# Two transformer layers on one core: the border from layer 0 to layer 1, with unordered scatters per expert, a separate pool for expert outputs, token loads moved ahead of list set-up, and first roots taken tile by tile

## The chip, the cores and the metric

The kernel runs on one core of a Trainium2 chip. A core has five engines that each work through a list of instructions of their own, in order: TensorE (PE in the profile; its weight loads are PEld), VectorE (DVE), ScalarE (ACT), GpSimd (POOL) and SyncE (SP, here only an issuer of transfers). They wait for each other through semaphores. Transfers run on 16 DMA engines; those that SP issues are in the profile's queue q1, those that POOL issues (the indirect ones, which take row numbers from memory) in q0. SBUF is the on-chip memory, PSUM the memory that TensorE writes to.

The metric is device time in microseconds (us). The kernel before takes 3005.03 us, the median of three runs (3000.24, 3005.03 and 3007.15).

## The reference, cut to what matters

`x` is 4096 tokens (2 x 2048) of 512 numbers in f32. Two layers follow each other; each is an attention to a short context and then a mixture of experts.

```python
x = x + attention_0(layernorm(x), ctx)            # 16 heads, 154 context rows
# layer 0, experts: each of 8 experts picks its 1024 best tokens
xf = layernorm(x).reshape(-1, 512)
scores = softmax(xf @ router_w + router_b)
G, idx = top_k(scores.T, 1024)                    # per expert
h1 = relu(xf[idx] @ w1 + b1)                      # 512 -> 2048
eo = h1 @ w2 + b2                                 # 2048 -> 512
y = zeros_like(xf).at[idx.reshape(-1)].add((eo * G[..., None]).reshape(-1, 512))
x = x + y
x = x + attention_1(layernorm(x), ctx)            # one head, 154 context rows
# layer 1, experts: each token picks 2 of 8 experts, plus a shared one
x = x + shared(layernorm(x)) + routed(layernorm(x))
```

A token can be picked by several experts of layer 0, but by one expert at most once.

## The kernel before, in words

The kernel is one program in four stages: attention of layer 0; choice of tokens and experts of layer 0; attention, shared expert and routing of layer 1; routed experts of layer 1. The change touches the end of the second stage and the start of the third.

**Experts of layer 0.** A block is half the tokens of one expert, 512 of them, so there are 16 blocks `b`. `hidden(b)` computes the first product, `outputs(b, b2_bc)` the second, both in a scheme that gets each pair of 2 x 2 block products from seven products and extra additions. `product` emits the matmuls (L709). While it emits them it counts ticks, and `after(n, fn)` puts other work into the engines' lists n ticks later; so the code itself fixes each engine's order (the stage is under a manual schedule for TensorE, DVE, ACT and POOL). SP is not in it: its order comes from the scheduler.

`outputs` works in two passes `p`, each of which makes two tiles of 128 tokens in one buffer `eo` of two halves (tag "eo", two buffers, in the pool `sm`). The last product of a pass, `p4`, completes tile `p + 2`. `finish` adds the bias `b2` on POOL (L928), scales by the gate on ACT three ticks later (`scale`, L895), and scatters two ticks after that (`scatter`, L900): an indirect transfer on POOL's queue that adds 128 rows of 2 KB to the rows of `xacc` in device memory that `idx` names. `xacc` holds the residual stream. Because all scatters write the same tensor, each one waits until the one before it has landed.

**The border.** When the pools of layer 0 close, their SBUF is given to the pools of layer 1, and a tile of layer 1 waits for whatever last used its place. SP then issues, in this order: seven loads that layer 1 needs throughout (L1046 to L1059: `kw`, `vp`, the two parts of `wsr`, `sb1_bc`, `ws2`, `sb2_bc`; here called the preloads), six small transfers that initialise rows of zeros and empty lists (L1090, L1093, L1097), and the tokens `x2[t]` from `xacc`, 256 KB a tile (`load`, L1135). Between them come the weights of the routed experts (`load_routed`, into `wall`), an expert per four steps. Each of SP's transfers uses one of eight semaphores in turn, and waits until the transfer eight places before it has landed.

**Attention and routing of layer 1.** `step(s)` emits the work of one step for a pipeline over 32 tiles; s runs from -10. A tile's layer norm is taken in three places: `stats(t)` on DVE (L1150, L1151) gives mean and variance; `roots(m)` takes the square root (ACT, L1156) and the reciprocal (DVE, L1157) for four tiles at a time; `norm3(t)` normalises (POOL, L1164). For the first four tiles that is `roots(-1)` in step -4, after all four statistics. Then TensorE transposes the tile (L1120), ACT copies it (L1122), TensorE computes the scores (`scores1`, L1172), and DVE takes their minimum (L1177), the first work of the step's softmax. The functions of ACT come in tables, and a change of table is an instruction of its own (ACT_TABLE_LOAD).

The set-up of the lists (`zrow`, `rank_of`, `io_p`, `ids`, `region`, `unused`, `csum`, `tri1`) stands before the steps: counters on POOL, conversions and zeros on DVE, and the six small transfers. `zrow` shares the tag "xn3" with the normalised tiles, which have two buffers.

Of the kernel before, what the change touches and what calls it, by code (L numbers as in the profile page):

```python
# [20 lines left out]
P = 128  # L21
# [3 lines left out]
TB = 512  # L25
# [30 lines left out]
def two_layers(ctx: ExitStack, tc: tile.TileContext, a, out):  # L56
# [66 lines left out]
    with (  # L123
# [373 lines left out]
    with tc.tile_pool(name="wm", bufs=4) as wm:  # L497
# [188 lines left out]
        HD2 = D // 2  # L686
        with (
            tc.tile_pool(name="sm", bufs=2) as sm,
            tc.tile_pool(name="pm", bufs=2, space=PSUM) as pm,
# [5 lines left out]
            def after(n, fn, *args):  # L695

                due.setdefault(now[0] + n, []).append((fn, args))
# [196 lines left out]
            def scale(eo, gate):  # L894
                nc.scalar.mul(eo, eo, gate)  # L895

            def scatter(b, t, eo):
                e, half = divmod(b, CAP // TB)
                col = half * TPB + t
                nc.gpsimd.indirect_dma_start(  # L900
                    out=xacc[:, :],
                    out_offset=bass.IndirectOffsetOnAxis(ap=idx[:, e, col : col + 1], axis=0),
                    in_=eo,
                    in_offset=None,
                    compute_op=ALU.add,
                )

            def outputs(b, b2_bc):
                e, half = divmod(b, CAP // TB)
                w2v = [blocks_of_w2(e, q) for q in range(4)]  # L910
                hsum = {}

                def hs(p, i):
# [13 lines left out]
                def finish(t, eo):  # L927
                    nc.gpsimd.tensor_tensor(eo, eo, b2_bc, ALU.add)  # L928
                    after(3, scale, eo, gates.pop((b, t)))
                    after(5, scatter, b, t, eo)  # L930

# [13 lines left out]
                for p in range(2):  # L945
# [3 lines left out]
                    def p_(h, m):  # L949
                        return product([[(h[:, j], m(j // 2)[:, j % 2]) for j in range(JF)]])[:, 0]  # L950
# [4 lines left out]
                    def w2t(i):  # L955
                        return lambda q: t2w[e, q][:, i]

                    u1, u2, u3, u23 = u_tiles(1)
                    u1, u2, u3, u23 = u1[:, 0], u2[:, 0], u3[:, 0], u23[:, :, 0]
                    eo = sm.tile([P, 2, D], F32, tag="eo", name="eo", bufs=2)  # L960
                    p1 = p_(a11, w2b(0))
# [70 lines left out]
    with ExitStack() as outer:  # L1032
# [42 lines left out]

        zrow = sf1.tile([P // 2, D], F32, tag="xn3", name="zrow")
        nc.vector.memset(zrow, 0.0)

        def iota1(shape, pattern, base_, mult, name):
            i = sf1.tile(shape, I32, tag=name + "_i", name=name + "_i", bufs=1)  # L1080
            nc.gpsimd.iota(i, pattern=pattern, base=base_, channel_multiplier=mult)
            f = wf.tile(shape, F32, name=name)
            nc.vector.tensor_copy(f, i)
            return f

        rank_of = iota1([P, E], [[-1, E]], E, 0, "rank_of")
        io_p = iota1([P, 1], [[1, 1]], 0, 1, "io_p")
        ids = iota1([P, SPLIT, 2], [[2 * P, SPLIT], [1, 2]], 0, 2, "ids")
        for G_ in groups:
            nc.sync.dma_start(G_.xn[G_.n : G_.n + P // 2, :], zrow)  # L1090
            G_.region = iota1([P, E], [[G_.n, E]], 0, 0, f"region{G_.g}")
            unused = iota1([2 * E, P], [[1, P]], 2 * G_.n, P, f"unused{G_.g}")
            nc.sync.dma_start(  # L1093
                G_.lists[0 : G_.rows, :].rearrange("(e r) c -> e r c", e=E),
                unused[0:E].unsqueeze(1).to_broadcast([E, G_.n // P, P]),
            )
            nc.sync.dma_start(G_.lists[G_.rows : G_.rows + E, :], unused[E : 2 * E])  # L1097
            G_.csum = wf.tile([P, E], F32, name=f"csum{G_.g}")
            nc.vector.memset(G_.csum, 0.0)
        tri1 = wf.tile([P, P], F32, name="tri1")  # L1100
        nc.gpsimd.affine_select(
            tri1, ones, pattern=[[1, P]], compare_op=ALU.is_gt, fill=0.0, base=0, channel_multiplier=-1
        )
        rank_bc = rank_of.unsqueeze(1).to_broadcast(SH)

        def first_highest(v, m, oh):

            m2 = sf.tile([P, TPB, 1], F32, tag="fh_m", name="fh_m")
            nc.vector.tensor_reduce(m, v, AX.X, ALU.max)
            nc.vector.tensor_tensor(oh, v, m.to_broadcast(SH), ALU.is_equal)  # L1110
            nc.vector.tensor_tensor(oh, oh, rank_bc, ALU.mult)
            nc.vector.tensor_reduce(m2, oh, AX.X, ALU.max)
            nc.vector.tensor_tensor(oh, oh, m2.to_broadcast(SH), ALU.is_equal)
# [45 lines left out]

        def norm3(t):  # L1160
            blk, i = divmod(t, TPB)
            mv, rstd, _ = event(blk - 1)
            x3n[t] = sf1.tile([P, D], F32, tag="xn3", name="xn3")
            nc.gpsimd.tensor_scalar(  # L1164
                x3n[t], x2[t], mv[:, 1, i, 0:1], rstd[:, 1, i : i + 1], ALU.subtract, ALU.mult
            )

# [184 lines left out]
        def block_of(m):  # L1352
            return 0 <= m < NB

        def step(s):
# [59 lines left out]
        def table(G_):  # L1415
# [16 lines left out]
            first = small([P, E], F32, "first")  # L1432
            nc.vector.tensor_scalar(past, end, io_p, None, ALU.is_le)
            nc.vector.tensor_tensor(first, past, n_t, ALU.mult)
# [3 lines left out]
            nc.vector.tensor_reduce(ex[:, 1:2], first, AX.X, ALU.add)  # L1438
            nc.vector.tensor_tensor(ex[:, 2:3], io_p, ex[:, 1:2], ALU.subtract)
            nc.vector.scalar_tensor_tensor(  # L1440
# [3 lines left out]

            nc.vector.tensor_scalar_add(ex[:, 3:4], io_p, float(G_.rows - 2 * G_.n // P))
            nc.vector.tensor_tensor(ex[:, 3:4], ex[:, 3:4], past[:, E - 1 : E], ALU.mult)
# [245 lines left out]
```

## Time and profile before

| What | Value |
|---|---|
| median of three runs | 3005.03 us |
| the profiled execution's own time | 3016.07 us |
| its span, first to last instruction | 3014.4 us |
| mean granted TensorE clock | 0.966 |
| TensorE busy (matmul) | 2778.1 us, 92% |
| DVE busy | 1547.0 us, 51% |
| POOL busy | 1216.7 us, 40% |
| ACT busy | 880.1 us, 29% |
| scatters to xacc | 64, of 1.57 us on POOL each, from 797.4 to 2312.8 us |

A line of the timeline gives the start, the length, the engine, the source line, the operation with "output <- input" by the program's names, the shapes and the count; in brackets stands how long the engine was idle before it and who released it. A line of the chain that ended last gives start, length and the work that the chain went through there. An engine's idle time matters only where that engine, or what waits for it, is on the path that sets the end. All times of a trace are counted from the start of the span.

### The profile page before, as it was taken

The numbers are of one execution on the slowest core, as the hardware profiler recorded it, in microseconds if no ns is written. First come the engines' busy times: TensorE is split into PE (matmuls) and PEld (weight loads), VectorE is DVE, ScalarE is ACT, GpSimd is POOL, SyncE is SP. The second block draws the span as 40 slices with busy tenths as digits, with TensorE's granted clock in tenths as the row PEclk, the third lists the DMA queues.
The fourth block names the chain that finished last, engine by engine and source line by source line (L and its number), as shares of the span: only waits on it lengthen the run. The fifth ranks groups of instructions, "written<-read, shape, count | busy, mean of one in ns | idle before, by whom it ended". The sixth has DMA issues, their size and how long they took to land. (4 is left out here: it accounts for less than half of the span.)

```text
span 3014.4 us, 38792 instructions
## 1 busy us (share of the span) xinstructions
PE 2778.1 (92%) x14262; PEld 2133.2 (71%) x14262; DVE 1547.0 (51%) x2933; ACT 880.1 (29%) x1854; POOL 1216.7 (40%) x986
## 2 busy tenths in 40 slices
PE   7889998867999999999999999999995888889995
PEld 4444554445888888888888888888885655567773
DVE  4677776544545435444454355443532555544355
ACT  2555554411122112212122112211220555432331
POOL 1445544403344424343334333432431555465552
PEclk9899999878999999999999999999998999899998
DMA  4011111161122231231222312312113642143387
GB/s 160 18 36 46 47 61 47 53 219 38 25 77 84 44 111 25 78 86 27 67 81 70 88 22 78 88 29 85 56 15 80 220 81 64 47 92 129 133 315 282
DMA packets 127083, 256.47 MB, mean 85 GB/s; under 512 B 16508, under 2 KB 22668, under 8 KB 126742
## 3 DMA queue, kind: packets, MB, share of 16 engines
q1 hardware_dynamic: 93232, 170.79, 16.9%
q0 software_dynamic: 29056, 74.81, 10.8%
q10 hardware_dynamic: 4608, 8.39, 0.7%
q8 instruction: 115, 1.88, 0.3%
q14 instruction: 72, 0.59, 0.1%
HBM read 176.09 MB, written 77.85 MB: 84 GB/s over the span
## 5 line engine op out<-in xcount | busy, mean ns | idle before, releaser
L831 ACT ACTIVATE H<-H,b_sb 128x256 f32<-128x256 f32 (+1 forms) x384 | 198.9, 571 | 563.0 <-DVE H L882 287.0
L928 POOL TENSOR_TENSOR eo<-eo,b_bc 128x512 f32<-128x512 f32 x64 | 96.4, 1506 | 647.4 <-DVE eo L974 585.4
L709 PE MATMUL prod<-w2q,H 128*128 128x256 f32 x1536 | 346.9, 379 | 0.0
L709 PEld LDWEIGHTS prod<-w2q,H 128*128 128x128 f32 x1536 | 289.5, 190 | 38.1
L312 POOL TENSOR_TENSOR pr<-pr,sm 128x616 f32<-128x616 f32 x128 | 155.2, 1213 | 275.5 <-DVE sm L311 249.7
L709 PE MATMUL prod<-xsum,sw 128*128 128x256 f32 x1024 | 245.4, 380 | 0.7 <-DVE xsum L792 0.7
L709 PE MATMUL prod<-xgT,w1q 128*128 128x256 f32 x1024 | 243.2, 380 | 0.0
L709 PE MATMUL prod<-xgT,sw 128*128 128x256 f32 x1024 | 243.1, 380 | 0.0
L709 PE MATMUL prod<-tw,hs 128*128 128x256 f32 x1024 | 234.5, 380 | 0.0
L817 POOL TENSOR_TENSOR sw<-w1q 128x512 f32<-128x512 f32 x128 | 189.6, 1481 | 84.3 <-PE prod L709 84.0
L709 PEld LDWEIGHTS prod<-xgT,w1q 128*128 128x128 f32 x1024 | 195.5, 191 | 26.8
L709 PEld LDWEIGHTS prod<-tw,hs 128*128 128x128 f32 x1024 | 192.8, 190 | 27.8 <-PE prod L709 2.5
L709 PEld LDWEIGHTS prod<-xsum,sw 128*128 128x128 f32 x1024 | 193.3, 190 | 26.7 <-POOL sw L817 1.0
L709 PEld LDWEIGHTS prod<-xgT,sw 128*128 128x128 f32 x1024 | 193.4, 190 | 25.7
L113 ACT COPY xgT<-pt 128x512 f32<-128x512 f32 x64 | 37.5, 585 | 431.7 <-PE pt L112 431.7
L900 POOL DMA_INDIRECT xacc<-eo,idx x64 | 100.6, 1572 | 153.0 <-DMA xacc<-eo,idx 92.1
L1513 PE MATMUL ph<-xgT,wc 128*128 128x128 f32 x1248 | 152.6, 275 | 7.4 <-DVE wc L1503 6.0
L289 DVE TENSOR_REDUCE mx<-sc 128x4 f32<-128x616 f32 x128 | 101.8, 795 | 105.5 <-PE sc L285 103.5
L1513 PEld LDWEIGHTS ph<-xgT,wc 128*128 128x128 f32 x1248 | 145.6, 192 | 9.0 <-issue 5.3
L1528 PE MATMUL po<-wall,h1r 128*128 x312 | 146.7, 593 | 1.7 <-issue 1.7
L1536 DVE TENSOR_TENSOR y<-po,wall 128x512 f32<-128x512 f32 x78 | 53.9, 691 | 144.1 <-PE po L1528 134.1
L1485 POOL DMA_INDIRECT xg<-xn,xrow x78 | 84.1, 1079 | 106.6 <-PE pt L1120 100.6
(296 smaller groups left out, 5156.9 us busy)
## 6 DMA issues: line engine op xcount, KB each, us to landing
w1q<-in_w SPq DMA_DIRECT2D x32, 1024.0 KB
w2q<-in_w SPq DMA_DIRECT2D x32, 1024.0 KB
y<-ys SPq DMA_DIRECT2D x40, 256.0 KB
xs<-row SPq DMA_DIRECT2D x32, 260.0 KB
x_sb<-in_x SPq DMA_DIRECT2D x32, 256.0 KB
x<-in_x SPq DMA_DIRECT2D x32, 256.0 KB
xacc<-x SPq DMA_DIRECT2D x32, 256.0 KB
x<-xacc SPq DMA_DIRECT2D x32, 256.0 KB
```

The lines of the kernel that those rows point to most:

```text
L113: nc.scalar.copy(dstT[:, :, ts(t, P)], pt)
L289: nc.vector.tensor_reduce(mx, sc[:, :, 0:TKV], AX.X, ALU.min)
L312: nc.gpsimd.tensor_tensor(pr, pr, sm.to_broadcast([P, 4, TKV]), ALU.mult)
L709: nc.tensor.matmul(ps[:, g, :], w, m, start=i == 0, stop=i == len(terms) - 1)
L817: nc.gpsimd.tensor_tensor(o, l, m, ALU.add if i == 0 else ALU.subtract)
L831: nc.scalar.activation(dst, src, AF.Relu, bias=b1_sb[:, e, f : f + 1])
L900: nc.gpsimd.indirect_dma_start(out=xacc[:, :], out_offset=bass.IndirectOffsetOnAxis(ap=idx[:, e, col : col + 1], axis=0), in_=eo, in_offse ...
L928: nc.gpsimd.tensor_tensor(eo, eo, b2_bc, ALU.add)
L1485: nc.gpsimd.indirect_dma_start(out=xg[r], out_offset=None, in_=G_.xn[:, :], in_offset=bass.IndirectOffsetOnAxis(ap=G_.xrow[:, i : i + 1], ...
L1513: nc.tensor.matmul(ph[:, c, :], wc[:, k * HE + c * P : k * HE + (c + 1) * P], x_[:, k, :], start=k == 0, stop=k == KC - 1,)
L1528: nc.tensor.matmul(po_[r], h[:, c, :], wflat[:, bass.ds(at + (W2_AT + c * D), D)], start=c == 0, stop=c == HE // P - 1)
L1536: nc.vector.tensor_tensor(y, po_.pop(r), wflat[:, bass.ds(at + B2_AT, D)], ALU.add)
```

## The change

1. *Scatters without order.* The scatters of one expert are declared free of dependences among each other. The scatter follows sooner: scaling after two ticks and scatter after three, in place of three and five, so that on POOL a tile's scatter stands before the other tile's bias add.
2. *Own memory.* `eo` moves from the pool `sm` to a pool of its own, `se`, that is opened first.
3. *The last tile of layer 0.* In the last pass of the last block, `finish_early` adds the bias and scales both finished parts (the right half of `eo`, and `u3`) before the last product; the last product's output is scaled and added to `u3` by one DVE instruction, and the scatter follows. A one-element memset of POOL stands between the last two scatters.
4. *Tokens first.* The set-up of the lists becomes a function, `lists_init`, that is called in step -4, after ten token loads and part of a weight load have been issued. `zrow` moves to the tag "xn4", and "xn3" gets three buffers.
5. *First roots tile by tile.* `first_tiles` takes statistics, root, reciprocal and normalisation of tiles 0 to 3 one after the other; the first three are normalised on DVE in place of POOL. A square root of one element (`warm`) ahead of the steps brings in the table.

The diff without what only moves or is re-indented:

```diff
         with (
+            tc.tile_pool(name="se", bufs=2) as se,
             tc.tile_pool(name="sm", bufs=2) as sm,
...
             def scatter(b, t, eo):
...
-                nc.gpsimd.indirect_dma_start(
+                sc_ = nc.gpsimd.indirect_dma_start(
...
+                tc.declare_no_dep(sc_.ins, group=f"xacc{e}", reason="an expert's tokens differ")
+                tc.add_to_no_dep_group(f"xacc{e}", sc_.ins)
...
                 def finish(t, eo):
                     nc.gpsimd.tensor_tensor(eo, eo, b2_bc, ALU.add)
-                    after(3, scale, eo, gates.pop((b, t)))
-                    after(5, scatter, b, t, eo)
+                    after(2, scale, eo, gates.pop((b, t)))
+                    after(3, scatter, b, t, eo)
+
+                def finish_early(eo, u3):
+
+                    gate = gates[b, TPB - 1]
+                    nc.vector.tensor_tensor(eo[:, HD2:D], eo[:, HD2:D], b2_bc[:, HD2:D], ALU.add)
+                    nc.vector.tensor_tensor(u3, u3, b2_bc[:, 0:HD2], ALU.add)
+                    scale(eo[:, HD2:D], gate)
+                    scale(u3, gate)
...
-                    eo = sm.tile([P, 2, D], F32, tag="eo", name="eo", bufs=2)
+                    eo = se.tile([P, 2, D], F32, tag="eo", name="eo")
...
-                    p4 = p_(a22, w2t(2))
-                    nc.vector.tensor_tensor(eo[:, 1, left], p4, u3, ALU.add)
-                    after(1, finish, p + 2, eo[:, 1])
+                    if last and p == 1:
+                        finish_early(eo[:, 1], u3)
+                        p4 = p_(a22, w2t(2))
+                        gate = gates.pop((b, TPB - 1))
+                        nc.vector.scalar_tensor_tensor(eo[:, 1, left], p4, gate, u3, ALU.mult, ALU.add)
+
+                        after(1, nc.gpsimd.memset, se.tile([P, 1], F32, name="pad", bufs=1), 0.0)
+                        after(1, scatter, b, TPB - 1, eo[:, 1])
+                    else:
+                        p4 = p_(a22, w2t(2))
+                        nc.vector.tensor_tensor(eo[:, 1, left], p4, u3, ALU.add)
+                        after(1, finish, p + 2, eo[:, 1])
...
-        zrow = sf1.tile([P // 2, D], F32, tag="xn3", name="zrow")
-        nc.vector.memset(zrow, 0.0)
...
+        def lists_init():
+            nonlocal rank_of, io_p1, ids, tri1
+            zrow = sf.tile([P // 2, D], F32, tag="xn4", name="zrow", bufs=3)
+            nc.vector.memset(zrow, 0.0)
...
-        def norm3(t):
+        def norm3(t, eng=nc.gpsimd):
             blk, i = divmod(t, TPB)
             mv, rstd, _ = event(blk - 1)
-            x3n[t] = sf1.tile([P, D], F32, tag="xn3", name="xn3")
...
+            x3n[t] = sf1.tile([P, D], F32, tag="xn3", name="xn3", bufs=3)
+            eng.tensor_scalar(x3n[t], x2[t], mv[:, 1, i, 0:1], rstd[:, 1, i : i + 1], ALU.subtract, ALU.mult)
+
+        def first_tiles():
+
+            mv, rstd, _ = event(-1)
+            for t in range(TPB + 1):
+                if t < TPB:
+                    stats(t, False)
+                    nc.scalar.activation(rstd[:, 1, t : t + 1], mv[:, 1, t, 1:2], AF.Sqrt, bias=eps_t)
+                if t > 0:
+                    nc.vector.reciprocal(rstd[:, 1, t - 1 : t], rstd[:, 1, t - 1 : t])
+                    if t < TPB:
+                        norm3(t - 1, nc.vector)
...
-            if tile_of(s + 7):
+            if s + 7 >= TPB and tile_of(s + 7):
                 stats(s + 7, False)
+            if s + 7 == TPB - 1:
+                first_tiles()
+                lists_init()
...
-            if i == 0 and -1 <= m <= NB:
+            if i == 0 and 0 <= m <= NB:
                 roots(m)
...
-            if tile_of(s + 3):
+            if s + 3 >= TPB - 1 and tile_of(s + 3):
                 norm3(s + 3)
...
         with tc.manual_schedule(engines={ET.PE, ET.DVE, ET.Activation}):
+
+            warm = sf.tile([P, 1], F32, name="warm", bufs=1)
+            nc.scalar.activation(warm, eps_t, AF.Sqrt)
```

In the order of the built program TensorE's list is the same before and after. On SP the six small transfers stand behind the tenth token load and the first piece of `wall`, and the first stores of normalised tiles stand up to two places earlier among the loads. On DVE the list's conversions stand between the third normalisation and the statistics of tile 4.

More of the change, by code (lines that the diff above doesn't have):

```diff
@@ L911, in outputs @@
                 hsum = {}
+                last = b + 1 == E * (CAP // TB)
                 def hs(p, i):
@@ L1074, in load_routed @@
             nc.sync.dma_start(w[:, B2_AT:WROW], a["rb2"][e].partition_broadcast(P))
-        zrow = sf1.tile([P // 2, D], F32, tag="xn3", name="zrow")
-        nc.vector.memset(zrow, 0.0)
[L1079 to L1095, printed above, removed]
-            )
-            nc.sync.dma_start(G_.lists[G_.rows : G_.rows + E, :], unused[E : 2 * E])
-            G_.csum = wf.tile([P, E], F32, name=f"csum{G_.g}")
-            nc.vector.memset(G_.csum, 0.0)
@@ L1100, in two_layers, with iota1 @@
[L1100 to L1104, printed above, removed]
+        rank_of = io_p1 = ids = tri1 = None
+        def lists_init():
+            nonlocal rank_of, io_p1, ids, tri1
+            zrow = sf.tile([P // 2, D], F32, tag="xn4", name="zrow", bufs=3)
+            nc.vector.memset(zrow, 0.0)
+            def iota1(shape, pattern, base_, mult, name):
+                i = sf1.tile(shape, I32, tag=name + "_i", name=name + "_i", bufs=1)
+                nc.gpsimd.iota(i, pattern=pattern, base=base_, channel_multiplier=mult)
+                f = wf.tile(shape, F32, name=name)
+                nc.vector.tensor_copy(f, i)
+                return f
+            rank_of = iota1([P, E], [[-1, E]], E, 0, "rank_of")
+            io_p1 = iota1([P, 1], [[1, 1]], 0, 1, "io_p")
+            ids = iota1([P, SPLIT, 2], [[2 * P, SPLIT], [1, 2]], 0, 2, "ids")
+            for G_ in groups:
+                nc.sync.dma_start(G_.xn[G_.n : G_.n + P // 2, :], zrow)
+                G_.region = iota1([P, E], [[G_.n, E]], 0, 0, f"region{G_.g}")
+                unused = iota1([2 * E, P], [[1, P]], 2 * G_.n, P, f"unused{G_.g}")
+                nc.sync.dma_start(
+                    G_.lists[0 : G_.rows, :].rearrange("(e r) c -> e r c", e=E),
+                    unused[0:E].unsqueeze(1).to_broadcast([E, G_.n // P, P]),
+                )
+                nc.sync.dma_start(G_.lists[G_.rows : G_.rows + E, :], unused[E : 2 * E])
+                G_.csum = wf.tile([P, E], F32, name=f"csum{G_.g}")
+                nc.vector.memset(G_.csum, 0.0)
+            tri1 = wf.tile([P, P], F32, name="tri1")
+            nc.gpsimd.affine_select(
+                tri1, ones, pattern=[[1, P]], compare_op=ALU.is_gt, fill=0.0, base=0, channel_multiplier=-1
+            )
@@ L1110, in first_highest @@
             nc.vector.tensor_tensor(oh, v, m.to_broadcast(SH), ALU.is_equal)
-            nc.vector.tensor_tensor(oh, oh, rank_bc, ALU.mult)
+            nc.vector.tensor_tensor(oh, oh, rank_of.unsqueeze(1).to_broadcast(SH), ALU.mult)
             nc.vector.tensor_reduce(m2, oh, AX.X, ALU.max)
@@ L1158, in roots @@
             nc.vector.scalar_tensor_tensor(nmr[:, h], mv[:, h, :, 0], -1.0, rstd[:, h], ALU.mult, ALU.mult)
-        def norm3(t):
+        def norm3(t, eng=nc.gpsimd):
             blk, i = divmod(t, TPB)
             mv, rstd, _ = event(blk - 1)
-            x3n[t] = sf1.tile([P, D], F32, tag="xn3", name="xn3")
-            nc.gpsimd.tensor_scalar(
-                x3n[t], x2[t], mv[:, 1, i, 0:1], rstd[:, 1, i : i + 1], ALU.subtract, ALU.mult
-            )
+            x3n[t] = sf1.tile([P, D], F32, tag="xn3", name="xn3", bufs=3)
[10 more added lines that the diff above has]
+                        norm3(t - 1, nc.vector)
         def scores1(t):
@@ L1432, in table @@
             first = small([P, E], F32, "first")
-            nc.vector.tensor_scalar(past, end, io_p, None, ALU.is_le)
+            nc.vector.tensor_scalar(past, end, io_p1, None, ALU.is_le)
             nc.vector.tensor_tensor(first, past, n_t, ALU.mult)
@@ L1438, in table @@
             nc.vector.tensor_reduce(ex[:, 1:2], first, AX.X, ALU.add)
-            nc.vector.tensor_tensor(ex[:, 2:3], io_p, ex[:, 1:2], ALU.subtract)
+            nc.vector.tensor_tensor(ex[:, 2:3], io_p1, ex[:, 1:2], ALU.subtract)
             nc.vector.scalar_tensor_tensor(
@@ L1443, in table @@
             G_.row_l = small([P, 1], U32, "row_l")
-            nc.vector.tensor_scalar_add(ex[:, 3:4], io_p, float(G_.rows - 2 * G_.n // P))
+            nc.vector.tensor_scalar_add(ex[:, 3:4], io_p1, float(G_.rows - 2 * G_.n // P))
             nc.vector.tensor_tensor(ex[:, 3:4], ex[:, 3:4], past[:, E - 1 : E], ALU.mult)
```

## The prediction

> **What bounds the kernel now.** I read the table of stretches first, then the waits of the stretch it singles out, then the timeline and the chain that ended last across that stretch. Columns of the table: stretch, its length, busy time and instruction count of PE, PEld, DVE, ACT and POOL, granted clock, DMA share, GB/s.
>
> ```profile
> 2200.00:2305.00 105.00, 105.00 (x488) 92.36 (x487) 34.73 (x46) 18.84 (x35) 26.14 (x19) 1.00 0.08 11
> 2305.00:2318.00 13.00, 0.32 (x2) 0.00 (x0) 0.66 (x2) 0.72 (x1) 4.69 (x6) 0.68 0.32 40
> 2318.00:2340.00 22.00, 0.00 (x0) 0.00 (x0) 6.64 (x25) 1.58 (x2) 3.23 (x9) 0.50 0.90 293
> 2340.00:2350.00 10.00, 9.21 (x36) 7.05 (x36) 2.49 (x12) 6.58 (x11) 6.14 (x3) 0.64 1.05 368
> ```
> From 740 to 2305 every stretch that I asked for shows TensorE busy for its whole length, as the first line does (105.00 of 105.00 us); there only its own work counts. Then it stands still for 34.7 us, with the clock down to half. That gap is the border between the two layers, and all four edits meet in it.
>
> The waits of that earlier part, read next, give POOL 92.1 us in which a scatter waited for the scatter before it (20 times, 6.6 at most). It is large, but all but its last few us lie under the gapless stretch. The timeline across the gap:
>
> ```profile
> 2301.70 3.62 PE L709 MATMUL prod<-tw,H 128*128 128x256 f32 x16
> ...
> 2307.27 1.55 POOL L900 DMA_INDIRECT xacc<-eo,idx  x1 [0.15 <-issue]
> ...
> 2317.66 0.34 SPq L1046 DMA_DIRECT2D kw<-kw_d  x1
> ...
> 2328.72 4.98 SPq L1135 DMA_DIRECT2D x<-xacc  x10
> ...
> 2331.47 0.69 DVE L1150 BATCH_NORM_STATS2 st<-x 128x6 f32<-128x512 f32 x1 [12.41 <-DMA x<-xacc]
> ...
> 2335.96 1.28 ACT L1156 ACT_TABLE_LOAD   x1 [28.09 <-DMA x<-xacc]
> ...
> 2337.87 6.20 POOL L1164 TENSOR_SCALAR xn<-x,mv,rstd 128x512 f32<-128x512 f32 x3 [18.77 <-DMA x<-xacc]
> ...
> 2340.01 1.11 PE L1120 MATMUL pt<-ident,xn 128*128 128x128 f32 x4 [34.69 <-POOL xn L1164]
> ...
> 2344.25 0.32 DVE L1177 CUSTOM_DVE_ANT_0 pr<-sc,bqk 128x154 f32<-128x154 f32 x1 [3.89 <-PE sc L1172]
> ```
> The gap is one chain. The last product ends at 2305.32; its output is biased, scaled and scattered in two ordered scatters; SP's first load of layer 1 starts at 2317.66; ten token loads start at 2328.72; the first statistics run at 2331.47; the roots of four tiles wait for four statistics and a table load; then POOL normalises for 2.07 us a tile. The first scores reach DVE at 2344.25. The chain that ended last says what holds the tokens back:
>
> ```profile
> 2312.81 4.71 DMA xacc<-eo,idx
> ...
> 2320.93 8.43 DMA sb_bc<-in_sb
> ```
> The last scatter lands at 2317.52. The seventh preload, sb2_bc, lands at 2329.36, 11.7 us after the first was issued, with the DMA engines 0.84 busy between 2317.6 and 2329.6. So the seven preloads (2.66 MB) are limited by transfer, and tokens queued behind them can't arrive before them.
>
> **The change part by part**, against the profiled span of 3014.4 us.
>
> *Scatters without order, before the last block.* A scatter now follows its own scaling, so POOL's 92.1 us go, and the second bias add of a pair stands behind the first scatter. Worth nothing: TensorE has no idle time there. The cover would fail if POOL's weight sums (L817) came late. In one block (1219 to 1238) the second scatter is issued at 1224.90, the two sums behind it end at 1228.97 and TensorE uses the first at 1234.70. In the new order I get that scatter at 1220.4 (first scatter 1216.4 when ACT's scaling ends, add 1218.0 to 1219.3, scaling), so the sums come 4 us earlier.
>
> *The last block.* The bias add of the last output goes to DVE ahead of the last product: two half adds (0.42 each by the L977 row), then two half scalings on ACT, all under TensorE's 3.62 us. POOL loses the 1.26 us add at 2305.86. The first scatter then starts when ACT's scaling ends (2303.70 + 0.72), at 2304.5 instead of 2307.27. One DVE instruction ends the product (2305.35 + 0.45 = 2305.8). The second scatter, the one that lands last, follows the first (2304.5 + 1.55, the pad and an issue gap of 0.15) at 2306.2 instead of 2312.81. With 1.55 us of issue and 3.16 to land it is there at 2310.9.
>
> *Own memory.* Before, the first preload waits for the last scatters, whose source lies in its place. In the changed program's list of waits it waits for DVE's last instruction instead: 2305.9 instead of 2317.66, 11.7 us earlier. Alone, the seven would be there at 2317.6. They now run beside two scatters. The last one alone kept the engines busy for 2.0 us (shares 0.24, 0.94 and 0.84 of the three us from 2314). Bounds: nothing, where they fill holes (the preloads leave 0.16), to 4.0 us, where each displaces its full share. I take 2.0, since 0.16 of 12 us is 1.9: preloads at 2319.6.
>
> *Tokens first.* Six small transfers (zero rows, empty lists; issues 2321.61 to 2327.86) move on SP behind ten token loads and a weight load. The first token load then needs only the last scatter (2310.9) and queues straight behind the preloads: about 0.9 us for 256 KB at 293 GB/s and 0.3 to be seen, instead of 2.1 after sb2_bc. First statistics at 2320.8, against 2331.47: **10.7 us** (8.7 to 12.7). What waits behind the moved six is token 10: they need DVE's zero rows (about 2327), so its load is issued near 2332 and lands near 2336. DVE wants it in step 3, near 2342. Covered by 6 us.
>
> *Roots tile by tile.* From the first statistics to the first scores on DVE: 12.8 us now. Afterwards, from that instant: statistics 0.83 a tile, four reciprocals 0.18, three normalisations on DVE 0.54 (the shorter of two DVE rows of that shape, 0.54 and 0.62), gaps included: 6.1 us; the moved zero rows and conversions (0.48 and about 0.9, by 2317.77 to 2319.06): 7.5; three more statistics: 10.0. On the other side ACT takes the fourth root at 5.5, copies the transposed tile to 6.1, and scores at half clock (2.42) end at 8.6. DVE is later: 10.0, **2.8 us** saved. Bounds: 0, if DVE's list drags as much as the old roots did, to 4.2, if only the scores bind. The square-root table is loaded while ACT waits anyway. Later steps keep their distance (3.5 and 4.3 us by 2344.25, 2347.78 and 2352.11). TensorE executes the same list, and the third xn buffer frees only POOL, which was two tiles ahead.
>
> Sum: 10.7 + 2.8 = 13.5 us. Span 3014.4 to 3000.9; the profiled run's 3016.07 to 3002.6. That run lies 11.0 above the median of the runs shown, so the same step gives 3005.03 - 13.5 = **2991.5**.
>
> [...] The table load took 1.28 us, and the square root followed 0.01 us behind it. [...]
>
> **The rivals.**
> 1. *Transfers take it back.* Preloads pay 4.0 us and DVE's list saves nothing, or a token load starves a step: gain 8.7 at the bounds, 4 with one starved step (4.2 us) more. For it: DMA share above 1.0 from 2340 to 2360. Against it: a step needs 256 KB in 4.2 us, 61 GB/s of some 370. About 3000.
> 2. *Nothing moves.* Another load holds the steps, token 10 for example landing at 2355 instead of 2336, and the gap ends where it did: 3005. Against it: before, token 10 was issued 7.5 us ahead of the first scores and nobody waited.
> 3. *Slower: the clock.* After the gap the clock stood at 0.50 until 2347, 7 us after TensorE's first work, which then filled 5.21 of 6.00 us. Now there is a burst of 1.1 us, a pause of 2.5, then scores. If this is too thin, steps run at half clock: 7.9 us (scores 2.42, the others doubled) instead of 4.2, so 3.7 a step. It decides from the fourth such step on; seven give 3017. Against it: from the scores on, work is as dense as before.
> 4. *Both bounds good*: 16.9 us, 2988.
>
> **How the numbers follow.** Forecast 0.76 (gain 9 to 15), rival 1 0.11, rival 2 0.05, rival 3 0.03, rival 4 0.05. A difference of 0.2%, 6 us, is about what a measurement of this kernel can tell from none. Faster: 0.76 + 0.05 + 0.07 of rival 1 = 0.88; same: 0.04 + 0.05 = 0.09; slower 0.03. The runs shown spread over 7 us, so the bounds (2988 to 2996) are widened by about 3.5 on each side: 2984.5 to 2999.5.
>
> **What would show it.** Two scatters back to back near 2306, the first preload at 2306, first statistics near 2321, four single roots with no table load between them, first scores on DVE near 2331, TensorE's gap near 18 us instead of 34.7, and equal spacing after. It is wrong if the preloads still start after the last scatter, if statistics start after 2323, if a step before the sixth waits for a token load, or if TensorE shows gaps before 2305.

## The result, and the profile after

The changed kernel takes 2991.57 us, the median of 17 runs (2987.07 to 2999.45); the kernel before takes 3003.38 in the same set (17 runs, 3000.24 to 3008.47). The ratio is 0.9959, 95% interval 0.9952 to 0.9966: 12.3 us faster (10.2 to 14.4). In another set of runs, with its own runs of the kernel before, the ratio was 0.9959 again (0.9945 to 0.9972). The forecast was 2991.5.

The table of stretches of the changed kernel, with the columns explained above:

```profile
2200.00:2306.00 106.00, 106.00 (x493) 93.37 (x492) 36.74 (x49) 18.85 (x36) 26.37 (x19) 1.00 0.08 11
2306.00:2310.00 4.00, 0.87 (x5) 0.41 (x3) 0.48 (x1) 2.26 (x4) 2.76 (x5) 1.00 0.33 77
2310.00:2318.00 8.00, 0.00 (x0) 0.00 (x0) 0.00 (x0) 0.00 (x0) 1.25 (x9) 0.61 1.06 288
2318.00:2325.00 7.00, 0.00 (x0) 0.00 (x0) 1.76 (x6) 0.42 (x2) 0.17 (x1) 0.50 0.97 338
2325.00:2332.00 7.00, 4.36 (x16) 3.56 (x16) 6.74 (x25) 2.52 (x5) 2.23 (x2) 0.50 0.71 228
```
TensorE is still busy for every microsecond up to its last product, and then stands still for 18.75 us instead of 34.69. The DMA engines, a third busy before while the scatters ran, are now at 1.06 from 2310 to 2318. The timeline of the changed kernel across the gap:

```profile
2303.25 3.62 PE L710 MATMUL prod<-tw,H 128*128 128x256 f32 x16
...
2303.79 0.41 DVE L940 TENSOR_TENSOR eo<-eo,b_bc 128x256 f32<-128x256 f32 x1
2303.97 1.37 POOL L933 TENSOR_TENSOR eo<-eo,b_bc 128x512 f32<-128x512 f32 x1 [15.53 <-DVE eo L987]
2304.12 1.50 DVE L941 TENSOR_TENSOR u<-u,b_bc 128x256 f32<-128x256 f32 x1
...
2305.65 0.51 ACT L896 ACTIVATE u<-u,gate 128x256 f32<-128x256 f32 x1 [0.91 <-DVE u L941]
2306.07 0.70 ACT L896 ACTIVATE eo<-eo,gate 128x512 f32<-128x512 f32 x1
...
2307.05 1.55 POOL L901 DMA_INDIRECT xacc<-eo,idx  x1 [1.71 <-ACT eo L896]
...
2307.54 0.34 SPq L1068 DMA_DIRECT2D kw<-kw_d  x1
...
2317.51 6.45 SPq L1161 DMA_DIRECT2D x<-xacc  x10
...
2323.14 0.69 DVE L1176 BATCH_NORM_STATS2 st<-x 128x6 f32<-128x512 f32 x1 [15.67 <-DMA x<-xacc]
...
2325.62 1.09 PE L1146 MATMUL pt<-ident,xn 128*128 128x128 f32 x4 [18.75 <-DVE xn L1190]
...
2328.59 2.42 PE L1208 MATMUL sc<-kw,xT 128*128 128x154 f32 x8 [1.89 <-ACT xT L1148]
...
2332.16 0.29 DVE L1213 CUSTOM_DVE_ANT_0 pr<-sc,bqk 128x154 f32<-128x154 f32 x1
```
And its chain that ended last (start, length, what):

```profile
2308.91 8.59 DMA xacc<-eo,idx
...
2318.85 4.28 DMA x<-xacc
```
The second of the two scatters is issued at 2308.91 and lands at 2317.50; only then is the first token load issued. Alone, before the change, the same transfer took 4.71. Everything below is told from the end E of layer 0's last product (start of its 16 matmuls plus 3.62: 2305.32 before, 2306.87 after), since that takes out what differs ahead of the border:

| us from E | before | changed | forecast |
|---|---|---|---|
| second scatter issued | +7.49 | +2.04 | +0.9 |
| second scatter landed | +12.20 | +10.63 | +5.6 |
| first preload | +12.34 | +0.67 | +0.6 |
| last preload landed | +24.04 | +15.4 | +14.3 |
| first statistics | +26.15 | +16.27 | +15.5 |
| first scores on DVE | +38.93 | +25.29 | +25.5 |

The chain goes through the scatter, because it releases the token loads. But a token load then stands on SP's queue behind what is left of the preloads. The seventh and the eighth of the token loads have to wait for the transfers eight places before them, `ws2` and `sb2_bc`. From the waits of SP's queue, and the eighth in the timeline:

```profile
SPq L1161 <- DMA ws<-in_sW: 1.2, 1, 1.2
SPq L1161 <- DMA sb_bc<-in_sb: 0.4, 1, 0.4
```
```profile
2322.31 0.32 SPq L1161 DMA_DIRECT2D x<-xacc  x1
```
So the last preload landed just ahead of 2322.31, at E+15.4. That is 4.8 us after the scatter and 0.8 ahead of the first statistics: it is the preloads that set the arrival of the first token.

The border is 13.64 us shorter. The two spans differ by more, 22.4, because the profiled execution of before was an unusual one. A second profiled execution of the kernel before shows it.

> The kernel before once more, unchanged, for a second profiled execution. In the profiled executions so far the changed kernel's gap is 13.6 us shorter, but from the first scores of layer 1 to the end there are 670.2 us before and 659.8 after, a further 10.3 us that the medians (11.8 apart) do not have. If those belong to that one execution (its own time is 3016 against a median of 3003), this one shows about 660 us for that stretch and a span near 3002. If they belong to the kernel, 670 again.

Its own time is 3003.18. The timeline gives its last product and its first scores, for a span of 3001.4:

```profile
2303.41 3.62 PE L709 MATMUL prod<-tw,H 128*128 128x256 f32 x16
...
2345.89 0.32 DVE L1177 CUSTOM_DVE_ANT_0 pr<-sc,bqk 128x154 f32<-128x154 f32 x1 [3.88 <-PE sc L1172]
```
The first scores stand at E+38.86, as in the first execution (38.93), but from there to the end it takes 655.5 us, against 670.2. Its first statistics stand at E+26.73 instead of E+26.15. So the border repeats within 0.1 us, its two parts within 0.7, and the rest of the span moves by 15; whole spans of single executions can't be compared here. From the first scores to the 32nd the steps take 244.35 us in this execution and 244.28 in the changed kernel.

### The profile page after: what moved, and what is told of

It reads as the page before. It is cut to its first block, busy times and chain, and to the rows that moved or that the text cites. A ratio compares the mean times of both kernels' runs of the same rounds, so it can differ in the third digit from the quotient of the medians.

```text
span 2992.0 us, 38786 instructions
## 1 busy us (share of the span) xinstructions
PE 2773.7 (93%) x14262; PEld 2134.2 (71%) x14262; DVE 1571.9 (53%) x2940; ACT 883.2 (30%) x1859; POOL 1200.7 (40%) x983
## 5 line engine op out<-in xcount | busy, mean ns | idle before, releaser
L933 POOL TENSOR_TENSOR eo<-eo,b_bc 128x512 f32<-128x512 f32 x63 | 110.2, 1749 | 647.0 <-DVE eo L987 647.0
L818 POOL TENSOR_TENSOR sw<-w1q 128x512 f32<-128x512 f32 x128 | 180.0, 1406 | 140.2 <-PE prod L710 139.9
L818 POOL TENSOR_TENSOR sw<-w1q,sw 128x512 f32<-128x512 f32 x64 | 83.0, 1296 | 111.0 <-PE prod L710 111.0
```

The source lines that it names most:

```text
L818: nc.gpsimd.tensor_tensor(o, l, m, ALU.add if i == 0 else ALU.subtract)
```

## The experiments

Each undoes or alters one thing in the changed kernel. Ratios are to the kernel before on the same chip; with intervals of 1.0 to 1.8 thousandths on either side (3 to 5 us) they tell large steps alone, so the small ones are read from E. On the chip of the first three runs the kernel before took 3003.67 us, on others 3003.34, 3020.09 and 3018.64.

Behind the first scores TensorE's clock adds a difference of its own. In five runs (order back, memory back, last block back, table late, early preloads) it is still at half when the scores of the second tile are due. The timelines of the run with the order back and of the changed kernel:

```profile
2335.52 2.39 PE L1206 MATMUL sc<-kw,xT 128*128 128x154 f32 x8
```
```profile
2333.53 1.31 PE L1208 MATMUL sc<-kw,xT 128*128 128x154 f32 x8
```
In these five the three steps behind the first scores take 12.9 to 13.2 us, in the nine other executions 11.9 to 12.1. So they pay about 1 us that the first scores don't show.

**The order of the scatters put back.**

```diff
-                tc.declare_no_dep(sc_.ins, group=f"xacc{e}", reason="an expert's tokens differ")
-                tc.add_to_no_dep_group(f"xacc{e}", sc_.ins)
```


> The changed kernel with one part undone: the scatters of an expert are ordered again, each waits for the one before it to land. Everything else as changed. Times are told from the end E of layer 0's last product. Theory 1 (the last scatter took 8.59 us in the changed kernel because it shared the DMA engines with the preloads; it was 4.71 alone): the first of the two is now the one beside the preloads and lands at about E+7 to E+9, the second is issued only then, on queues that the preloads still fill, and lands at E+14 to E+17; first token load then, first statistics at E+18 to E+20 against E+16.3, so 2 to 4 us slower than the changed kernel, some 9 us faster than before. Rival (two scatters back to back slow each other, the preloads do not): the first lands at E+4.9, the second at E+9.7, first statistics at E+15.5 to E+16, no slower than the changed kernel. In both, no idle time of TensorE ahead of E although POOL's waits of scatter for scatter (92 us before) are back.

2994.16 us, ratio 0.9969 (0.9958 to 0.9981). From its waits, its table of stretches and its timeline:

```profile
POOL xacc L901 <- DMA xacc<-eo,idx: 91.1, 27, 6.3
```
```profile
740.00:2300.00 1560.00, 1560.00 (x7527) 1370.03 (x7526) 740.10 (x1006) 315.23 (x594) 569.79 (x430) 1.00 0.23 60
```
```profile
2303.59 3.62 PE L710 MATMUL prod<-tw,H 128*128 128x256 f32 x16
2307.39 1.55 POOL L901 DMA_INDIRECT xacc<-eo,idx  x1 [1.71 <-ACT eo L896]
...
2316.48 1.58 POOL L901 DMA_INDIRECT xacc<-eo,idx  x1 [6.84 <-DMA xacc<-eo,idx]
2322.31 4.61 SPq L1159 DMA_DIRECT2D x<-xacc  x10
2325.08 0.69 DVE L1174 BATCH_NORM_STATS2 st<-x 128x6 f32<-128x512 f32 x1 [17.28 <-DMA x<-xacc]
```
All 91.1 us in which POOL waits for an earlier scatter are back, and TensorE is busy for 1560.00 of 1560.00 us all the same. A single scatter beside the preloads, with no other scatter in flight, holds back the next one until 9.09 us after its own issue (2307.39 to 2316.48); the next one, issued when most preloads are through, takes 5.8. So the preloads slow it, and the rival falls. First statistics at E+17.9, first scores 1.6 us later than in the changed kernel, and another 1 us is lost behind them with the clock: these 2.6 us are all that the missing order is worth, at the last pair.

**The memory of the expert outputs put back.**

```diff
-                    eo = se.tile([P, 2, D], F32, tag="eo", name="eo")
+                    eo = sm.tile([P, 2, D], F32, tag="eo", name="eo", bufs=2)
```


> The changed kernel with one part undone: the expert outputs lie again in memory that layer 1's tiles take over, so the first preload has to wait for the last scatters. Theory 1 (preloads slow the scatter, 8.59 us beside them): with the preloads held back, the second scatter, issued at about E+2, takes 4.7 us as before the change and lands at E+6.8; the first preload starts there (E+6.9 against E+0.7), seven preloads take 11.7 us as before, token loads follow; first statistics at E+19.5 to E+20.5 against E+16.3: 3 to 4 us slower than the changed kernel. Rival (the two scatters slow each other): the second still takes 8.6 us, the first preload starts at E+10.7, first statistics at E+23.5 to E+24.5, 7 to 8 us slower than the changed kernel.

2998.22 us, ratio 0.9977 (0.9968 to 0.9987). Its chain, and its stretches while the scatters run alone and while the preloads do:

```profile
2309.99 5.11 DMA xacc<-eo,idx
2316.05 8.30 DMA wsr<-in_sW
2324.74 4.64 DMA x<-xacc
```
```profile
2308.00:2315.10 7.10, 0.00 (x0) 0.00 (x0) 0.49 (x1) 0.00 (x0) 3.22 (x3) 0.84 0.59 74
2315.30:2324.70 9.40, 0.00 (x0) 0.00 (x0) 0.00 (x0) 1.49 (x2) 1.15 (x8) 0.50 0.88 256
```
Without preloads beside it the second scatter takes 5.11 us and lands at E+7.15. The first preload starts at E+7.29, the tokens follow behind it, first statistics at E+21.5 and first scores at E+30.6: 5.3 us lost, somewhat more than expected, since the tokens now stand behind all of the preloads. The stretches also give the price of a scatter: two of them hold the 16 engines for 0.59 of 7.10 us, 4.2 us, while they move 74 GB/s; the preloads move 256 GB/s at 0.88.

**The last block put back.**

```diff
-                    if last and p == 1:
+                    if False:
```


> The changed kernel with one part undone: the last output's bias and scaling come after the last product again (POOL adds, ACT scales, then the scatter), as for every other output. Theory (the border chain starts with the second scatter): it is issued 1.3 us (POOL's add) plus 0.5 us (scaling) plus gaps later, at E+2.7 to E+4.0 against E+2.0, and first statistics follow by as much: 0.7 to 2.8 us slower than the changed kernel. Rival (by then the preloads hold the tokens, not the scatter): the scatter starts later and first statistics stay at E+16.3.

2994.22 us, ratio 0.9972 (0.9961 to 0.9982). The second scatter is issued at E+3.27 instead of E+2.04, the tokens at E+11.96 instead of E+10.64, first statistics come at E+17.49 and first scores at E+26.52: 1.2 to 1.3 us later at each place. But the first preload starts later too, at E+3.01 instead of E+0.67, because it waits for the scaling on ACT in place of DVE's last instruction. From the waits of SP's queue:

```profile
SPq L1068 <- ACT eo L896: 156.4, 1, 156.4
```
So the run shows what the edit is worth, 1.2 us to the first scores. It doesn't show that the scatter carries it: the expectation's rival, that the preloads hold the tokens, isn't excluded here, and the landing of the last preload speaks for it.

**The lists ahead of the tokens.**

```diff
+        lists_init()
         def first_highest(v, m, oh):
...
                 first_tiles()
-                lists_init()
```

> The changed kernel with one part undone: zero rows, rank tables and empty lists are made and sent ahead of the token loads again, as before. Times are told from the end E of layer 0's last product; the changed kernel has first statistics at E+16.3 and first scores on DVE at E+25.3, 9.0 apart. Theory 1 (the six small transfers ahead on the queue are worth the 1 to 2 us that the prediction put into its tokens term): token loads are issued and served later, first statistics at E+17.5 to E+19; DVE's list between statistics and scores is 1.4 us shorter (the zero rows and conversions are done earlier), so 7.6 to 8 apart, and the scores come 0 to 1.5 us later than in the changed kernel. Rival (the tokens wait for the last scatter anyway, so the small transfers fit ahead of it at no cost): first statistics stay at E+16.3 and the scores come 1.0 to 1.4 us earlier than in the changed kernel.

Ratio 0.9972 (0.9962 to 0.9982). Token loads are issued at E+15.31, first statistics come at E+18.25, first scores 7.92 us later at E+26.17. So the order is worth 2.0 us at the statistics and 0.9 at the scores; the other 1.1 it gives back, because zero rows and conversions now stand on DVE between the two.

**The four roots together, the table late, and both.**

```diff
-                first_tiles()
+                for t in range(TPB):
+                    stats(t, False)
+                roots(-1)
...
-            if s + 3 >= TPB - 1 and tile_of(s + 3):
+            if tile_of(s + 3):
                 norm3(s + 3)
```


> The changed kernel with one part undone: the roots of the first four tiles are taken together after four statistics, and POOL normalises them, as before. The table stays loaded ahead and the lists stay behind the tokens. Theory 1 (the saving of 3.8 us from first statistics to first scores comes from the single roots): 11.5 to 12.5 apart again, against 9.0, with first statistics unchanged at E+16.3; 2.5 to 3.5 us slower than the changed kernel. Rival (it comes from the table loaded ahead, 1.28 us, and from the tokens that arrive closer together): 9.0 to 10.5 apart, at most 1.5 us slower.

```diff
-            warm = sf.tile([P, 1], F32, name="warm", bufs=1)
-            nc.scalar.activation(warm, eps_t, AF.Sqrt)
```


> The changed kernel without its small root ahead of the first statistics, so that the square-root table is loaded when the first root is due; single roots stay. From first statistics to first scores on DVE the changed kernel takes 9.0 us, the run with the four roots together 10.4, the kernel before 12.8. Theory (the table load of 1.28 us stood on that path and was 1 to 1.3 of the 3.8 us saved): 10.0 to 10.3 apart. Rival (DVE's own list, which is late by 1.2 us, covers it): 9.0 to 9.3 apart, and then the table is worth nothing by itself. First statistics at E+16 to E+16.3 in both.

> The four roots together and POOL's normalisation back, and the table loaded late as well: both parts of the changed first roots undone, while the lists stay behind the tokens. Theory (roots 1.3, table 1.3, and the rest of the 3.8 us from tokens that arrive closer together): 11.4 to 11.9 apart, first statistics at E+16 to E+16.3. Rival (the table is hidden, and tokens alone make the rest): 10.4 apart as with the roots alone.

Ratios 0.9955 (0.9938 to 0.9973), 0.9969 (0.9956 to 0.9981) and 0.9973 (0.9959 to 0.9987). From first statistics to first scores they take 10.35, 10.12 and 11.76 us; the changed kernel takes 9.02 and the one before 12.78. The timeline of the run with the table late:

```profile
2323.18 0.69 DVE L1176 BATCH_NORM_STATS2 st<-x 128x6 f32<-128x512 f32 x1 [15.53 <-DMA x<-xacc]
...
2324.23 1.28 ACT L1198 ACT_TABLE_LOAD   x1 [17.28 <-issue]
...
2325.53 0.48 ACT L1198 ACTIVATE rstd<-mv,eps_t 128x1 f32<-128x1 f32 x2
```
The load stands on the path and costs 1.10 of its 1.28 us. Of the 3.76 saved, the single roots are 1.33, the table 1.41 on top of them, and 1.02 is left, with both undone: the tokens of the first four tiles arrive closer together, since DVE no longer waits between them (0.94 before the third in the kernel before). The second execution of the kernel before agrees: DVE waits 0.29 there and the stretch is 12.13, so 3.11 are saved and 0.37 is left. My theory that the roots make it was wrong by more than half.

**Preloads under layer 0.** The seven go into a pool opened ahead of the others, meant to lie over the place of the `w1` tiles, which TensorE reads for the last time at about E-48. In the second version `lists_init()` moves to step 1.

```diff
     with ExitStack() as outer:
+        early = outer.enter_context(tc.tile_pool(name="early", bufs=1))
+        kwb, vpb = [], []
+        for b in range(B):
+            kwb.append(early.tile([P, KC, TKV], F32, tag="kx", name="kw1", bufs=2))
+            nc.sync.dma_start(kwb[b], kw_d[:, :, ts(b, TKV)])
...
         wh = outer.enter_context(tc.tile_pool(name="wh", bufs=1))
```

> The changed kernel with the seven preloads of layer 1 put into memory that layer 0 no longer uses some 50 us ahead of its last product, so that they lie under TensorE's work and nothing runs beside the last scatters. Theory 1 (the preloads stretch the last scatter from 4.7 to 8.6 us and then hold the token loads): the second scatter, issued at E+2.0, lands at E+6.8 to E+7.3, as in the run with the old memory; the first token is there 2.8 us later as before the change, first statistics at E+9.5 to E+10.1 against E+16.3, first scores 9.0 later at E+18.5 to E+19.1; 6 to 7 us faster than the changed kernel, about 2985. Rival (two scatters of 256 KB slow each other, or the loads of routed weights that remain do it): the scatter still takes 8.6 us, first statistics at E+13.4, 3 us faster than the changed kernel, about 2988.7.

> The kernel with the early preloads, and the making of zero rows and empty lists moved behind two more steps, off DVE's and POOL's list ahead of the first scores. Theory (DVE was late for the first scores by 1.2 us, because it ran zero rows and conversions first): first statistics as in the kernel with early preloads, first scores 7.8 to 8.2 us after them instead of 9.0, about 1 us faster, some 2984. Rival (token 10, whose load has to wait for the zero rows, or POOL's normalisations behind the lists, come late): a step between the second and the eighth is stretched by as much as is won, no faster.

Ratios 0.9955 (0.9938 to 0.9973) and 0.9951 (0.9936 to 0.9966). The edit didn't do what it was to do. From the waits of SP's queue and from the timeline of the first version:

```profile
SPq L1059 <- PE prod L710: 144.8, 1, 144.8
```
```profile
2303.83 3.62 PE L710 MATMUL prod<-tw,H 128*128 128x256 f32 x16
2304.07 1.32 SPq L1059 DMA_DIRECT2D kw<-kw_d  x2
...
2309.49 1.55 POOL L901 DMA_INDIRECT xacc<-eo,idx  x1 [0.19 <-issue]
2318.46 4.80 SPq L1170 DMA_DIRECT2D x<-xacc  x10
```
And from its chain:

```profile
2309.49 8.82 DMA xacc<-eo,idx
```
The first preload waited 144.8 us and started at E-3.4, when TensorE had done with the last product but one. That one reads `w2` tiles, not `w1`; both lie in one pool. Whether the wait covered the whole pool or the new one reached into the place of `w2`, the runs don't show. So the preloads again ran beside the scatter, which took 8.82 us. They were through earlier, though: the first statistics came 3.1 us after the first token load's issue instead of 5.6, at E+14.10 instead of E+16.27. So 2.2 us of the changed kernel's border are the preloads ahead of the tokens on the queue, with a scatter as slow as ever. The first scores came at E+23.14, 2.15 us better, of which the clock takes 1.1 back in the three steps behind. The version with the late lists takes 8.08 us from statistics to scores instead of 9.04: what DVE ran in between was on the path, worth 1.0. Its scatter took 9.60 us and its first statistics came at E+14.89, so its first scores, at E+22.97, are only 0.2 earlier.

**Tokens ahead of the preloads.** The other way to keep the scatter alone is to put the preloads behind the tokens.

```diff
+        def load_shared(s):
+            if s == -7:
+                nc.sync.dma_start(kw, kw_d)
+            if s == -3:
+                nc.sync.dma_start(vp, vp_d)
+            if s == -1:
+                ...
-            for s in range(-10, NT + 14):
+        with tc.manual_schedule(engines={ET.PE, ET.DVE, ET.Activation, ET.SP}):
+            for s in range(-10, 0):
+                step(s)
+        with tc.manual_schedule(engines={ET.PE, ET.DVE, ET.Activation}):
+            for s in range(0, NT + 14):
```
`load_shared(s)` is called in each step after the token load, and `lists_init()` in step 1. SP's queue is under the manual schedule for the first ten steps, so that the code fixes its order too.

> The changed kernel with layer 1's order on SP's queue turned round: four token loads, kw, three token loads, vp, two token loads, then wsr, sb1, ws2 and sb2; zero rows and lists are made two steps later, as in the run with early loads. So nothing runs beside the last scatters, and nothing lies between them and the tokens. Theory (the preloads stretch the scatter from about 5 to 8.6 us and then hold the tokens): the second scatter, issued at E+2.0, lands at E+7.3 as with the old memory; first statistics 2.8 us later, at E+9.8 to E+10.4 against E+16.3; kw, 1.7 MB into the queue, is there at about E+14, ahead of TensorE's need at E+15.4; first scores on DVE at E+18 to E+19 against E+25.3; the steps after keep their distance; 6 to 7.5 us faster than the changed kernel. Rival (the preloads that now come later take it back: kw or vp late, or a token behind them): first statistics at E+10 too, but the first scores at E+21 or later, or the first eight steps stretched, and 0 to 4 us faster than the changed kernel.

> The changed kernel once more, unchanged, on the same chip as the kernel with the tokens ahead of the preloads, for a direct comparison and a second profiled execution. If the border does what the first execution showed, first statistics at E+16.3 and first scores at E+25.3 again, within 0.5 us, whatever the rest of the span does; ratio to the kernel before within 0.995 to 0.997.

2984.38 us, ratio 0.9932 (0.9919 to 0.9945), beside 2991.22 and 0.9959 (0.9945 to 0.9972) for the changed kernel on the same chip. The timeline of the new version:

```profile
2304.89 3.62 PE L710 MATMUL prod<-tw,H 128*128 128x256 f32 x16
...
2310.54 1.55 POOL L901 DMA_INDIRECT xacc<-eo,idx  x1 [0.19 <-issue]
2315.80 1.76 SPq L1166 DMA_DIRECT2D x<-xacc  x4
...
2318.70 0.70 DVE L1181 BATCH_NORM_STATS2 st<-x 128x6 f32<-128x512 f32 x1 [9.59 <-DMA x<-xacc]
...
2326.61 0.32 DVE L1218 CUSTOM_DVE_ANT_0 pr<-sc,bqk 128x154 f32<-128x154 f32 x1 [1.00 <-PE sc L1213]
```
The second scatter takes 5.08 us, the tokens are loaded from E+7.29 and seen 2.9 us later, first statistics stand at E+10.19 and first scores at E+18.10. On the same chip the changed kernel has E+15.94 and E+24.96. That is 6.9 us, the difference of the two medians (6.84). Of these, 5.75 are there at the first statistics; the other 1.1, from statistics to scores (7.91 us instead of 9.02), go with the lists made later, as in the run above. Against the run with early preloads the statistics come 3.9 us earlier: nearly all of that is the stretch of the scatter, 8.82 us there and 5.08 here. DVE now waits 1.00 us for the scores instead of being late for them, and from the first scores to the 32nd it takes 244.38 us, so the preloads that come later hold up nothing. This kernel beats both.

## Why the prediction was right

The sum came out: 13.64 us at the border, and 13.90 between the second executions of the two kernels, against 13.5. The medians are 11.8 apart, and the interval of 10.2 to 14.4 holds all of these. That the time came within 0.1 us of 2991.5 is luck: the kernel before took 1.65 us less than in the runs that the forecast started from, and the medians moved 1.7 less. The two large terms were off in opposite directions in the first executions (9.88 for 10.7 and 3.76 for 2.8); between the second ones they are 10.79 and 3.11, so the split between them is known to about 0.9 us only.

*Scatters without order, worth nothing before the last block*: right, as the run with the order put back shows, 91.1 us of waits and a TensorE without a gap.

*The last block*: the second scatter was put at E+0.9 and came at E+2.04. The term "two half adds (0.42 each)" was mis-sized: the first took 0.41 us, the second 1.50, while POOL's add ran from 2303.97 to 2305.34. The scaling of `u` on ACT had to wait for it, and the scaling of the other output, which releases the first scatter, stood behind that in ACT's list.

*Its landing*: "1.55 us of issue and 3.16 to land" is the term that was furthest off. It came from a scatter alone. Beside the preloads the same transfer takes 8.59 us, and it landed at E+10.6 instead of E+5.6. The runs agree: 8.82 and 9.60 with the early preloads, 5.11 and 5.08 without preloads beside it. The sum didn't suffer, because the first token waited longer for the preloads. Where no preload was left ahead of the tokens, the first statistics came 2.8 to 2.9 us after the first token load's issue (2.77 with the order back, 2.90 with the tokens first, 2.94 with the lists first); that would have been E+13.4 to E+13.6 here, and they came at E+16.27.

*Own memory*: right. The first preload started where it was put (E+0.67 for E+0.6), and the tokens queued straight behind the preloads, as forecast. From the first preload's start to the last one's landing it takes 14.8 us instead of 11.7, so 2.0 us for contention were 3.1, within the bounds of nothing to 4.0, and the last preload landed at E+15.4 for E+14.3.

*Tokens first*: 9.88 us saved against 10.7. Behind what is left of the preloads it takes 5.63 us from issue to first statistics instead of 2.75 before. Token 10 was loaded in time: the first five steps are 3.25, 4.49, 4.20, 4.20 and 4.96 us apart, against 3.53, 4.33, 4.20, 4.21 and 4.95.

*Roots tile by tile*: 3.76 us against 2.8. DVE is the later one, as forecast (TensorE ends its scores at 2331.01, DVE turns to them at 2332.16), but its list took 9.0 us, not 10.0. The name of the term says too much: 1.33 belong to the roots and 1.41 to the table that is loaded ahead. With the table late the load took 1.28 us, the root started 0.02 us behind it, and leaving it on the path cost 1.10.

*The rivals*: transfers took back 1.1 us more than forecast, the later landing of the last preload, and no step starved. (The gain with one starved step, 8.7 less 4.2, is 4.5 us, not 4; about 3000 stands.) The clock (rival 3) decided nothing between the two kernels: the three steps behind the first scores take 11.94 us in the changed one and 12.06 before. Its rows stand in the last section. That nothing moves is excluded.

## What to carry to other kernels

Where a border waits for one last small transfer, keep bulk loads away from it. They cost twice here: beside the scatter they stretched it (3.9 us at the first statistics), and ahead of the tokens on the queue they held them (2.2). So the loads belong behind the first consumers' data and ahead of their own need. A chain that goes through the scatter doesn't show the second cost; the time from a load's issue to its first reader does (5.63 us instead of 2.8 to 2.9). Waits on an engine that has slack, 92 us of them here, are worth what the last of them is worth. Read such a border from the last product, not from whole spans: here its length to the first scores repeats within 0.4 us, while the rest of the span moves by up to 15. Then read a few steps further, where the clock cost 1 us in five of the runs.

## What the runs showed of the hardware

A scatter that adds 256 KB to scattered rows took 4.7 to 5.8 us with few other transfers, 8.6 to 9.6 beside the preloads. Two of them hold the DMA engines for 4.2 us at 74 GB/s.

A DVE add of two operands in SBUF that started 0.18 us ahead of a POOL add of two operands took 0.41 us. The next of the same shape, started 0.15 us after the POOL add, took 1.50 and ended 0.28 us after it. In seven other executions they took 0.41 to 0.42 and 1.49 to 1.50. Why the second takes longer, the runs don't show.

The granted clock fell to half 4.0 to 4.9 us after E in all fourteen profiled executions, and the stretch at half was a whole number of times 3.413 us, the length of the shortest one behind the border (2516.55 to 2519.97 in the first execution of the changed kernel): 6 times in both executions of the changed kernel (20.48 us), 11 times in both of the kernel before (37.55), 4 times with the tokens first (13.65), 6 to 9 times in the other runs. So the time from TensorE's first work to full clock isn't fixed. It was 5.3 to 8.0 us in nine executions and 11.5 to 12.1 in the five named above. The microsecond in which it came back, of the changed kernel (first work at 2325.62), of the kernel with the tokens first (2321.18) and of the one with the order back (2327.57):

```profile
2332.00:2333.00 1.00, 0.00 (x0) 0.00 (x0) 0.96 (x5) 0.51 (x3) 0.00 (x0) 0.88 0.52 95
```
```profile
2327.00:2328.00 1.00, 0.74 (x5) 0.24 (x3) 1.00 (x2) 0.98 (x4) 0.00 (x0) 0.98 1.00 282
```
```profile
2339.00:2340.00 1.00, 1.00 (x3) 0.34 (x2) 0.00 (x0) 0.13 (x2) 0.49 (x1) 0.89 0.67 205
```
By these mean clocks, and 0.50 in the microsecond ahead of each, it was back at 2332.24, 2327.04 and 2339.22, after 6.6, 5.9 and 11.65 us; the changed kernel even gets it in a microsecond in which TensorE does nothing. In the last 3.41 us of the stretch TensorE worked for 2.71 to 3.41 us (3.04 in the first execution of the changed kernel, 3.30 in that of the kernel before), in each earlier 3.41 us of it for 2.74 at most. Whether this work brings the full clock back, and how much of it is enough, the runs leave open: 2.71 us came ahead of the full clock once, and 2.74 twice didn't.

Sets of runs differ, each of them on one chip: the same kernel before took 3003 to 3004 us in three sets and 3019 to 3020 in two. In the latter the first statistics came at E+16.0 to E+16.2 where nothing ahead of them was altered, as elsewhere, while the steps from the first scores to the 32nd took 254.5 to 256.5 us instead of 244.3 to 249.2. The clock goes with it. These steps in the second execution of the changed kernel, and in the run with the lists first:

```profile
2332.03:2576.30 244.27, 212.18 (x1000) 146.06 (x1000) 153.50 (x493) 129.29 (x256) 134.33 (x119) 0.99 0.43 116
```
```profile
2330.58:2585.51 254.93, 223.21 (x1004) 152.21 (x1002) 143.35 (x493) 129.53 (x256) 134.34 (x119) 0.96 0.37 110
```
TensorE is busy 11 us longer with the same work at a lower mean clock; it is at half for 22 to 28 us of these steps in the six runs of the two slower sets, for 3.5 to 18.7 in the other eight executions. Why the clock falls more often there, the runs don't show.
